# Four table rows, and not two, loaded by SP behind each step of the sums of a graph-attention kernel

## The chip, the core and the metric

The kernel runs on one core of a Trainium2 chip. The core has five engines that work side by side, each through its own queue of instructions in order: TensorE (PE, matrix products; its weight loads are shown apart as PEld), VectorE (DVE), ScalarE (ACT), GpSimd (POOL) and SyncE (SP), which computes nothing and starts transfers. SP, ACT and POOL can all start DMA transfers, which 16 DMA engines carry out. An engine that meets an instruction whose input is not ready stops there, and everything behind it in its queue waits too.

The metric is the time of one execution on the device, in microseconds (us). Three runs of the kernel before took 1981.16, 1981.94 and 1984.87 us; the median is 1981.94 us. One more execution was profiled.

## The reference

The graph has 12,500 nodes with 128 features each and 200,000 edges with 64 features each. The edges come sorted by their target node. The computation is one layer of graph attention with four heads of 32:

```python
h = jnp.maximum(_layernorm(x, axis=-1), 0.0)
h = (node_features @ W_node.T).reshape(num_nodes, H, HD)      # node_features is the h above
e = (edge_features @ W_edge.T).reshape(num_edges, H, HD)
att = jnp.sum(jnp.concatenate([h[src], h[tgt], e], -1) * a, axis=-1)
att = jnp.where(att > 0, att, 0.2 * att)
m = jnp.maximum(segment_max(att, tgt), 0.0)
ex = jnp.exp(att - m[tgt])
denom = segment_sum(ex, tgt) + (num_edges - deg)[:, None] * jnp.exp(-m)
h_prime = segment_sum((ex / denom[tgt])[:, :, None] * h[src], tgt)
out = x + h_prime
```

What matters for this change is `h[src]`: every edge needs the row of its source node, and sources are random. A row holds 137 floats (548 bytes): the four heads' values, four columns of ones, a count and the source's share of the attention logit.

## The kernel before

The edges are cut into groups of 512 places (511 edges and one place for what the group before hands on), four chunks of 128 places to a group (`J`) and four groups to a quad (`QG`). There are 392 groups and 98 quads, numbered 0 to 97. A chunk is 128 rows of the table, one to each partition.

**Stages.** Up to about 100 us the kernel computes the table of node rows in DRAM, while the source inputs of the first four and a half quads are gathered and later converted on the spot. Then it goes over the quads. For each, `all_logits` (L898) makes the attention logits in four steps, one a group; `softmax` (L617) turns the logits of a whole super-quad (two to four quads) into weights; and `sums` (L821) multiplies the gathered rows by the weights and adds them up by target in four steps, with `divide` (L871) for the finished nodes. `together` (L169) interleaves such parts by hand, a step of each in turn: a quad's sums run beside the logits of a quad about five ahead. This order is written out in the code (a manual schedule); no planner moves anything.

**Where the rows come from.** `gather` (L149, its instruction L160) loads one chunk with one indirect DMA, which POOL issues; the rows land in `ga_all`, which has room for eight quads (`QUADS`). So POOL may run ahead of the sums by eight quads and no more.

Some chunks are taken from POOL and loaded row by row, 128 plain DMAs each, by ACT (the last chunk, j = 3, of some groups) and by SP (j = 2). `loaded_by_row` (L714) is a generator: each `next` issues one row's DMA. Which chunks these are is fixed ahead by the rate:

```python
def rows_for(a_quad, j, soonest):                              # L137
    for k in range(nq):
        q = soonest - -(k + 1) * P // a_quad
        if q < nq and quads[q][1] == QG and whole(quads[q][0] + QG - 1):
            by_row[q, QG - 1, j] = k
    return a_quad, j
sync_rows = rows_for((BEHIND_LOGITS + BEHIND_HOT) * QG, J - 2, SYNC_FROM + 6)   # L147
```

With `a_quad` rows a quad, chunk k is that of quad 8 + the rounded-up value of 128 (k + 1) / `a_quad`, as long as this lies below 98. `a_quad` is also the number of addresses that one register load brings to the engine: at every `a_quad`-th row of a chunk `windows` (L507) loads that many byte offsets from `at_row` into SP's registers; a row is then a register move and a DMA (L736). `at_row` is made by one small DVE instruction from `of` (L722, a 512-byte load by SP). The loaded chunk stands in one of three buffers (`ROW_BUFS`), and `take_rows` (L750) lets ACT copy it into `ga` at the head of `all_logits`.

**SP's queue.** SP issues nearly all other transfers, in program order: for each quad the targets `db` (L326, two buffers; each load waits until DVE has read the buffer's last content), the edge features `ea` (L321), and, through `issue` (L519, its DMA L523), four windows of the side table `pw`, four blocks of node inputs `xw` and four blocks of results `out_dram`; for each super-quad the edge order `dr` (L551). A step of the sums issues one `xw`, one `out_dram` and then the rows:

```python
issue("inputs", "results", *(["inputs"] * 3 if q == nq - 3 else []))   # L867, in sums
load_rows(by_sync, q, BEHIND_HOT)                                      # L868
```

A step of the logits issues one `pw` and then `load_rows(by_sync, q, BEHIND_LOGITS)` (L908). In the last step of a quad's logits the `db` of the quad after next comes between. The SP rows begin at quad 2 (`SYNC_FROM`). An `out_dram` waits for DVE's addition of the result (`res`, L892), and that addition waits for the quad's `xw`. The writes of `out_dram` may overlap, so each also waits for the one before to land.

Of the kernel before, what the change touches and what calls it, by code (L numbers as in the profile page):

```python
# [38 lines left out]
QUADS = 8  # L39
ROWS_FROM, ROWS_AHEAD, ROW_BUFS = 6, 7, 3  # L40
BEHIND_COUNT, BEHIND_SUMS, BEHIND_QUAD = 5, 1, 4
SYNC_FROM, BEHIND_LOGITS, BEHIND_HOT = 2, 3, 2
SETS = max(NODE_T, QG * J)
PAD = 1 << 20

# [1172 lines left out]
```

## Time and profile before

| What | Value |
|---|---|
| median of three runs | 1981.94 us |
| the profiled execution's own time | 1978.93 us |
| span in the profile, first to last instruction | 1976.9 us |
| PE, DVE, ACT, POOL busy | 70%, 67%, 22%, 75% of the span |
| chunks gathered by POOL | 1463 from the table, 72 from the inputs |
| rows loaded by ACT, by SP | 2304 (18 chunks), 1664 (13 chunks) |
| granted TensorE clock, mean | 0.539 |

Busy time counts instructions that compute; POOL's indirect DMAs count too, since POOL itself writes their descriptors. Instructions that issue a plain DMA, load a register or wait are not counted, so SP has no busy figure at all: what it does is read from its queue ("SPq" in the rows, "ACTq" for ACT's). In the views of waits a row names the engine and the line that waited, what released it, the sum in us, how often, and the longest. In the timeline a row gives start, duration and what ran; several like instructions in a row are merged, with the small gaps between them, and a time in square brackets is the idle time ahead with its releaser.

### The profile page before, as it was taken

To read this page: it belongs to the slowest core of one execution; us is meant where nothing else is said; L and a number is where in the kernel's file an instruction comes from. 1 tells how busy PE (TensorE), PEld (TensorE's weight loads), DVE (VectorE), ACT (ScalarE), POOL (GpSimd) and SP (SyncE) were. 2 spreads that over 40 slices of the span, in tenths; PEclk is the share of its full clock that TensorE was granted. 3 is DMA by queue.
4 is the path that set the end of the run, shared out by engine and by line. 5 is a ranking of instruction groups with operands and counts; after the bars stand their busy time and mean duration, and the time that the engine had idled before them with its cause. 6 is when DMAs were issued, how large, how long until landed. Compare 5 with 4: busy or idle time off the path is not lost. (4 is left out here: it accounts for less than half of the span.)

```text
span 1976.9 us, 35316 instructions
## 1 busy us (share of the span) xinstructions
PE 1384.9 (70%) x7327; PEld 1247.0 (63%) x7327; DVE 1329.2 (67%) x3297; ACT 426.4 (22%) x1563; POOL 1478.6 (75%) x1578
## 2 busy tenths in 40 slices
PE   6577777777776667667757666667676666777876
PEld 5466777667665656656656565566575655676765
DVE  7676767776775766656747656667576565777876
ACT  6664111211111111111111111111111111111222
POOL 7777777777777777777777777777777777777774
PEclk8877555555555555555555555555555555555557
DMA  7654666566665555565555645555656455565541
GB/s 255 207 146 117 159 153 150 138 151 150 151 156 142 145 138 137 131 144 139 135 138 135 149 123 138 136 143 131 146 129 149 123 149 126 137 153 131 150 103 35
DMA packets 201161, 280.05 MB, mean 142 GB/s; under 512 B 83352, under 2 KB 150839, under 8 KB 193104
## 3 DMA queue, kind: packets, MB, share of 16 engines
q1 hardware_dynamic: 145518, 166.49, 31.6%
q0 software_dynamic: 49120, 107.44, 23.6%
q10 hardware_dynamic: 6306, 3.85, 0.9%
q14 instruction: 156, 1.28, 0.2%
q8 instruction: 61, 1.00, 0.2%
HBM read 254.26 MB, written 23.30 MB: 140 GB/s over the span
## 5 line engine op out<-in xcount | busy, mean ns | idle before, releaser
L160 POOL DMA_INDIRECT ga<-table,srci x1463 | 1391.9, 951 | 448.1 <-issue 389.2
L864 PE MATMUL acc<-ga,hot 128*97 128x137 f32 x2352 | 646.4, 446 | 103.0 <-ACT ga L837 69.9
L864 PEld LDWEIGHTS acc<-ga,hot 128*97 128x97 f32 x2352 | 515.8, 277 | 124.4 <-ACT ga L837 83.6
L575 PEld LDWEIGHTS <-at 80*128 80x128 bf16 x1568 | 213.7, 164 | 384.0 <-DVE at L569 362.2
L578 PE MATMUL lg<-wblk,ea 128*128 128x8 f32 x1568 | 405.9, 356 | 0.0
L575 PE MATMUL lg<-pw,at 80*128 80x12 bf16 x1568 | 169.8, 181 | 314.5 <-DVE at L569 313.3
L578 PEld LDWEIGHTS lg<-wblk,ea 128*128 128x128 f32 x1568 | 378.4, 306 | 0.0
L788 ACT COPY pt<-acc 97x137 f32<-97x137 f32 x392 | 107.4, 274 | 819.2 <-PE acc L787 539.1
L787 PE MATMUL acc<-ga,hot 128*97 128x137 f32 x784 | 261.9, 437 | 27.5 <-ACT ga L785 27.0
L569 DVE TENSOR_TENSOR at<-const_ps,db 80x512 bf16<-80x512 f32 x392 | 267.2, 682 | 8.6 <-DMA db<-in_dst_dram 2.7
L844 DVE TENSOR_TENSOR ga<-ga,ex_ps 128x528 f32<-128x528 f32 x392 | 268.3, 685 | 0.6 <-DVE st L587 0.3
L781 DVE TENSOR_TENSOR ga<-acc,facs 1x132 f32<-1x132 f32 x391 | 115.7, 296 | 207.9 <-ACT pt L788 194.7
L787 PEld LDWEIGHTS acc<-ga,hot 128*97 128x97 f32 x784 | 193.5, 280 | 42.7 <-ACT ga L785 42.1
L599 DVE TENSOR_TENSOR U<-st,ga 128x64 f32<-128x64 f32 x98 | 26.4, 269 | 272.5 <-DMA ga<-table,srci 241.3
L857 DVE TENSOR_TENSOR hot<-const_ps,slot 128x320 f32<-128x320 f32 x384 | 183.1, 477 | 0.0
L785 ACT COPY ga<-acc 1x1 f32<-1x1 f32 x391 | 59.9, 153 | 328.4 <-DVE ga L781 283.0
L892 DVE TENSOR_TENSOR res<-res,xw 80x512 f32<-80x512 f32 (+2 forms) x100 | 67.1, 671 | 44.0 <-DMA xw<-in_x_dram 41.1
L160 POOL DMA_INDIRECT ga<-in_x_dram,srci x72 | 68.8, 956 | 23.1 <-issue 18.3
L888 DVE TENSOR_TENSOR res<-pt,const_ps 80x512 f32<-80x512 f32 (+2 forms) x103 | 67.6, 657 | 4.1 <-DVE const_ps L884 0.3
L691 PE MATMUL ex_ps<-ident,ex 64*128 64x64 f32 (+2 forms) x112 | 18.2, 310 | 53.0 <-ACT ex L678 53.0
L417 PE MATMUL row_ps<-wcat,hT 128*128 128x137 f32 x198 | 38.9, 345 | 21.2 <-DVE tgt L423 9.3
L417 PEld LDWEIGHTS row_ps<-wcat,hT 128*128 128x128 f32 x198 | 33.0, 239 | 26.8 <-ACT hn L248 16.6
(139 smaller groups left out, 1028.4 us busy)
## 6 DMA issues: line engine op xcount, KB each, us to landing
db<-in_dst_dram SPq DMA_DIRECT2D x98, 640.0 KB
ea<-in_edge_t_dram SPq DMA_DIRECT2D x98, 512.0 KB
by_row<-table ACTq DMA_DIRECT2D x2304, 0.5 KB
by_row<-table SPq DMA_DIRECT2D x1664, 0.5 KB
ga<-table,srci POOLq DMA_INDIRECT x1463
xw<-in_x_dram SPq DMA_DIRECT2D x392, 40.0 KB
out_dram<-res SPq DMA_DIRECT2D x392, 40.0 KB
pw<-side SPq DMA_DIRECT2D x392, 1.9 KB
```

What stands on the lines that cost most here:

```text
L160: nc.gpsimd.indirect_dma_start(out=ga[:, i, j, 0:width], out_offset=None, in_=rows, in_offset=bass.IndirectOffsetOnAxis(ap=srci[:, g0 + i, ...
L417: nc.tensor.matmul(row_ps[:, t, :ROW], hT[:, t, :], wcat, start=True, stop=True)
L569: nc.vector.tensor_tensor(at[:, i, :], node_ps[0:SPAN, g0 + i:g0 + i + 1].to_broadcast([SPAN, GE]), db[:, i, :], op=OP.is_equal)
L575: nc.tensor.matmul(lg[:, i, j].rearrange("p k h -> p (k h)"), at[:, i, j * P:(j + 1) * P], sw, start=i + j == 0, stop=False, skip_group_ch ...
L578: nc.tensor.matmul(lg[:, i, 2 * w:2 * w + 2, 0, :], ea[:, i, w, :], wblk, start=False, stop=True, skip_group_check=True)
L781: nc.vector.tensor_tensor(ga[0:1, i, 0, 0:H * HW].rearrange("p (h w) -> p h w", w=HW), before[WIN:WIN + 1, 0:H * HW].rearrange("p (h w) -> ...
L787: nc.tensor.matmul(acc, hot[:, i, 0, :], ga[:, i, 0, :], start=False, stop=True)
L788: nc.scalar.copy(pt[:, i, :], acc)
L844: nc.vector.tensor_tensor(val, val, weight.unsqueeze(3).to_broadcast([P, J, H, HW]), op=OP.mult)
L857: nc.vector.tensor_tensor(hot[:, i, :, 0:SPAN], lane_ps.unsqueeze(1).to_broadcast([P, J, SPAN]), slot[:, g, :].unsqueeze(2).to_broadcast([ ...
L864: nc.tensor.matmul(acc, hot[:, i, j, :], ga[:, i, j, :], start=j == 1, stop=False)
L888: nc.vector.tensor_tensor(res[:, :n, :].rearrange("p g (h d) -> p g h d", d=HD), val[:, :, :, 0:HD], share_ps[0:R, :n, :].unsqueeze(3).to_ ...
```

## The change

A constant is changed: behind each step of the sums SP loads four rows and not two. As a logits step still loads three, `a_quad` for SP becomes (3 + 4) x 4 = 28 and not 20, and by the rule of `rows_for` the chunks that SP loads become nineteen (k = 0 to 18: the last is that of quad 95) and not thirteen. One register load now brings 28 addresses and not 20. The six further chunks, and the places of all nineteen, are left out of what POOL gathers. ACT's chunks stay as they are.

```diff
 BEHIND_COUNT, BEHIND_SUMS, BEHIND_QUAD = 5, 1, 4
-SYNC_FROM, BEHIND_LOGITS, BEHIND_HOT = 2, 3, 2
+SYNC_FROM, BEHIND_LOGITS, BEHIND_HOT = 2, 3, 4
```

## The prediction

> **What bounds the kernel now.** I read the page first. Its chain of work that ended last covers less than 1% of the span and says nothing here, so I went to POOL's timeline, to DVE's waits by stretch, and to SP's queue.
>
> ```profile
> PE 1384.9 (70%) x7327; PEld 1247.0 (63%) x7327; DVE 1329.2 (67%) x3297; ACT 426.4 (22%) x1563; POOL 1478.6 (75%) x1578
> L160 POOL DMA_INDIRECT ga<-table,srci x1463 | 1391.9, 951 | 448.1 <-issue 389.2
> ...
> 1000.96 0.94 POOL L160 DMA_INDIRECT ga<-table,srci  x1 [0.30 <-issue]
> 1002.20 0.94 POOL L160 DMA_INDIRECT ga<-table,srci  x1 [0.30 <-issue]
> 1003.45 0.95 POOL L160 DMA_INDIRECT ga<-table,srci  x1 [0.30 <-issue]
> ...
> 1932.53 0.94 POOL L160 DMA_INDIRECT ga<-table,srci  x1 [0.31 <-issue]
> ```
>
> 75% busy looks like slack, but each chunk has 0.30 us before it that no wait explains: POOL starts a chunk every 1.25 us to its last at 1932.53. POOL is saturated. A quad is 16 chunks less 28/128 for ACT and 20/128 for SP, 15.63 chunks or 19.5 us. Whether the rest keeps up is in DVE's waits, from 257 to 621 us (first two rows) and from 621 to 1720 us (the third):
>
> ```profile
> DVE res L892 <- DMA xw<-in_x_dram: 38.4, 15, 4.8
> DVE U L599 <- DMA ga<-table,srci: 6.0, 2, 5.3
> ...
> DVE U L599 <- DMA ga<-table,srci: 225.4, 37, 10.4
> ```
>
> Two regimes. After 621 us the consumers (PE, DVE, ACT) wait for POOL's rows. Before, they hardly do, and wait for `xw`, which SP loads. POOL began its gathers at the start and is ahead; the consumers catch up. What SP waits for, in the same two stretches:
>
> ```profile
> SPq L523 <- DMA out_dram<-res: 18.9, 25, 2.8
> ...
> SPq L523 <- DVE res L892: 166.2, 49, 6.0
> SPq L523 <- DMA out_dram<-res: 13.8, 23, 1.2
> ```
>
> In the first, SP never waits for DVE, only for its own writes to land; in the second it waits 166 us for DVE. So SP sets the pace of the catch-up. Its pace per quad is the spacing of the `db` loads, one a quad (the number behind x counts them):
>
> ```profile
> L326 SPq DMA_DIRECT2D db<-in_dst_dram x21: 369/416/1210, 257.6 to 604.1; - x21
> 621.18 0.42 SPq L326 DMA_DIRECT2D db<-in_dst_dram  x1
> ...
> 257.57 0.42 SPq L326 DMA_DIRECT2D db<-in_dst_dram  x1
> 273.75 0.41 SPq L326 DMA_DIRECT2D db<-in_dst_dram  x1
> ...
> 281.01 0.56 SPq L736 DMA_DIRECT2D by_row<-table  x2
> 281.67 0.32 SPq L523 DMA_DIRECT2D pw<-side  x1
> 282.08 2.43 SPq L736 DMA_DIRECT2D by_row<-table  x3
> ...
> 286.61 0.87 SPq L736 DMA_DIRECT2D by_row<-table  x3
> 287.57 0.32 SPq L523 DMA_DIRECT2D xw<-in_x_dram  x1
> ...
> 289.53 0.42 SPq L326 DMA_DIRECT2D db<-in_dst_dram  x1
> ```
>
> 21 quads from 257.57 to 621.18 are 17.3 us each. Two clean ones, without `dr` and with hardly a wait, take 16.18 and 15.78 us: SP works all the time. SP therefore needs some 16.3 us of work a quad (17.3 less the 1.0 of waits above, 21 us in 21 quads with the small ones) against POOL's 19.5. That margin of 3.2 us is what the change spends.
>
> **The change, part by part.**
>
> *Off POOL.* Six chunks at 1.25 us: 7.5 us less. If POOL stayed the bound, this would be the whole result; its pace becomes 15.56 chunks, 19.4 us a quad.
>
> *Onto SP's queue, eight rows a quad.* A group of three rows takes 0.87 us and the next entry starts 0.10 later: 0.32 a row. With the stalls that the stretch's rows contain I take 0.34: 8 x 0.34 = 2.7 us.
>
> *The register loads.* They are not counted as busy, and hide in the 2.43 against 0.87 of the groups above.
>
> ```profile
> L509 SPq TENSOR_LOAD <-at_row x91: 526/1448/1632, 128.8 to 1718.9; - x91
> L509 ACTq TENSOR_LOAD <-at_row x90: 1190/1981/2182, 269.3 to 1815.4; - x90
> L729 DVE TENSOR_SCALAR at_row<-of x31: 203/216/460, 128.5 to 1742.1; 1x128 int32<-1x128 int32 x31
> L755 ACT COPY ga<-by_row x31: 287/305/307, 339.4 to 1897.0; 128x137 f32<-128x137 f32 x31
> ```
>
> (minimum, median, maximum in ns). SP's 20 addresses cost 1.45 us, and 8 cost 0.53; ACT already loads 28, for 1.98 (16 for 1.19). A chunk now needs 6 x 1.45 + 0.53 = 9.2 us over 6.4 quads, 1.44 a quad; then 4 x 1.98 + 1.19 = 9.1 over 4.57 quads, 1.99. That is 0.55 more. Fewer loads save nothing, since the price goes by the address.
>
> *Small things.* Six more `of` loads on SP, 0.02 us a quad. Six more `at_row` on DVE (1.3 us) and copies on ACT (1.8 us): beside other work, as DVE idles a third of the span and ACT more; without that cover they would cost those 3.1 us. The bytes moved are the same. A chunk's last row is still issued about three quads before its use, so ACT's wait in `take_rows` stays short.
>
> *SP's pace.* 16.3 + 2.7 + 0.55 + 0.02 = 19.6 us. The waits for landing writes shrink, as two rows (0.65 us) now stand between the writes in addition: the 25 waits average 0.76, and I keep 0.1 to 0.3 a quad. I take **19.7 us**. From below: the mean of the clean quads, 15.98, plus 3.2 (rows at 0.32) gives 19.2; from above: 17.3 with every old wait kept, plus 3.27, gives 20.6. The row nearest is the 21-quad spacing, so I stay near its work, 16.3.
>
> So SP falls behind POOL's 19.4. What is late next is everything that is issued behind the rows: `xw`, on which DVE's addition at L892 waits, then `pw`, `ea` and `db`, for PE and DVE. The consumers never catch up, POOL runs into the eight-quad limit and waits for the sums to free `ga`: its lost 7.5 us buy nothing.
>
> One page weighs the other way. The Trainium skill, DMA: Bandwidth & Descriptors, section "Issuing engines are not separate DMA queues", says that starting DMAs from several engines saves only the sequencer's time, "which is usually small relative to the DMA itself". By that SP's share would not count and the answer would be POOL's saving, the second case below. This trace disagrees about "small": 128 rows and their addresses occupy SP some 53 us, where POOL takes 1.25 us for the chunk.
>
> *The sum.* I date SP's last row, then add the rest.
>
> ```profile
> L736 SPq DMA_DIRECT2D by_row<-table x117: 227/233/287, 130.1 to 256.9; - x117
> L736 SPq DMA_DIRECT2D by_row<-table x420: 227/234/335, 258.1 to 620.5; - x140
> L736 SPq DMA_DIRECT2D by_row<-table x1127: 227/234/922, 621.7 to 1728.7; - x188
> ...
> 239.58 0.37 SPq L523 DMA_DIRECT2D xw<-in_x_dram  x1
> 244.06 0.34 SPq L523 DMA_DIRECT2D out_dram<-res  x1
> ...
> 1804.01 0.27 DVE L599 TENSOR_TENSOR U<-st,ga 128x64 f32<-128x64 f32 x1
> 1829.42 0.27 DVE L599 TENSOR_TENSOR U<-st,ga 128x64 f32<-128x64 f32 x1
> ...
> DVE U L599 <- DMA ga<-table,srci: 5.0, 2, 4.5
> ```
>
> Before 257.57 us SP has issued 117 rows; seven quads of logits made 84 of them and the sums 33, which double: 150. They lengthen the start by 0 to 12 us; waits like the 4.1 us ahead of 244.06 absorb part, so I take 4: SP passes the same place at 262. Of 19 x 128 = 2432 rows 2282 are left, 81.5 quads at 28. At 19.7 us the last row goes out at 262 + 1606 = 1868, not 1728.7. That is in the logits of quad 90.5, which stand between 1804 and 1829 in the trace of before: at 1817, 160 us ahead of the end of the span. In these 160 us the rows are gone, but the consumers have little to gain: the last row above says that from 1800 us on DVE waits only 5 us for POOL. I take 158. Span 1868 + 158 = 2026; with the 2.0 us that the profiled execution has around its span (1978.93 against 1976.9) 2028. The runs' median is 3 us above that execution, within what I can't resolve; I leave 2028.
>
> **The rivals.**
>
> *SP still fits; POOL stays the bound: faster.* It decides at a pace of SP of 19.0, where 262 + 1549 + 158 equals POOL's span of 1969. For it: in the second stretch SP has 3.0 us of waits a quad for DVE (166 us in 56 quads), as much as the change adds. Against it: these waits exist because consumers stand and wait for POOL; that needs the catch-up, which ran on a margin now gone. Time: 1978.93 - 7.5 = 1971.
>
> *SP and POOL tie.* At 19.1 to 19.2 SP loses little more than POOL gains: 1979 to 1986.
>
> *More issue contention.* ACT and SP together issue 56 rows a quad and not 48; single issues of SP's rows already take up to 0.92 us and not 0.23. At 20.5 us a quad: 262 + 1671 + 158 + 2 = 2093.
>
> **How the numbers follow.** Every 0.1 us of pace is 8 us of time. The forecast's case, 19.2 to 20.05, has 0.71 and its own range is 1987 to 2057. POOL-bound has 0.14, the tie 0.05, contention beyond 20.05 has 0.10. The range reaches into the first and the last: 1973 to 2065. Faster by over 0.2% (about what a measurement of this kernel can tell from no change) is 0.13, within it 0.06, slower 0.81.
>
> **What would show it.** Right: `db` loads about 19.7 us apart from 260 us to the end of SP's rows near 1870; hardly a wait of SP for DVE's `res`; DVE waiting for `xw` all along; the 225 us of DVE's wait for gathered rows nearly gone; POOL with idle times over 0.3 us released by PE (acc), where before there is none. Each chunk at 1.25 us still, 1457 of them. Wrong: SP's wait for `res` still there after 700 us, and POOL's last chunk about 7 us earlier. My weakest term is SP's work a quad, whose pieces are tenths of a microsecond, multiplied by 81.5.

## The result, and the profile after

The changed kernel takes 2043.06 us (median of six runs, 2039.74 to 2046.49), the kernel before 1984.28 us beside it (median of six, 1981.16 to 1985.72). The ratio is 1.0305, with a 95% interval of 1.0291 to 1.0319: slower by 3%, where 2028 us was forecast with a range of 1973 to 2065.

From the page of the changed kernel: the span and the engines' busy time, then the groups of POOL's gathers and of DVE's addition of the node inputs, and the rows that SP loads.

```profile
span 2044.7 us, 36881 instructions
PE 1379.1 (67%) x7327; PEld 1246.6 (61%) x7327; DVE 1328.9 (65%) x3303; ACT 427.0 (21%) x1569; POOL 1473.9 (72%) x1572
...
L160 POOL DMA_INDIRECT ga<-table,srci x1457 | 1387.2, 952 | 463.4 <-issue 379.5
...
L892 DVE TENSOR_TENSOR res<-res,xw 80x512 f32<-80x512 f32 (+2 forms) x100 | 67.0, 670 | 345.1 <-DMA xw<-in_x_dram 292.1
...
by_row<-table SPq DMA_DIRECT2D x2432, 0.5 KB
```

All busy sums are as before, within some microseconds, and POOL gathers six chunks less at the same 0.95 us each. Nothing computes longer; the added time is waiting. Where it arises is seen in DVE's waits. The first row is from 257 to 621 us, the other two from 621 to 1880 us:

```profile
DVE res L892 <- DMA xw<-in_x_dram: 70.4, 15, 8.6
...
DVE res L892 <- DMA xw<-in_x_dram: 220.8, 43, 8.5
DVE U L599 <- DMA ga<-table,srci: 0.4, 1, 0.4
```

The first regime of the kernel before, in which DVE waits for `xw`, now lasts to the end of SP's rows. The second, with its 225 us of waits for gathered rows, is gone: the consumers never reach POOL. SP's queue is shown next: a piece of its timeline, its `db` loads, its rows and its address loads, then its waits. The first row of waits is from 257.5 to 1880 us, the second over the whole span, and the last is the same row over the whole span of the kernel before:

```profile
945.61 0.32 SPq L523 DMA_DIRECT2D pw<-side  x1
946.02 2.88 SPq L736 DMA_DIRECT2D by_row<-table  x3
949.00 0.32 SPq L523 DMA_DIRECT2D xw<-in_x_dram  x1
949.41 0.38 SPq L523 DMA_DIRECT2D out_dram<-res  x1
949.88 1.20 SPq L736 DMA_DIRECT2D by_row<-table  x4
951.18 0.32 SPq L523 DMA_DIRECT2D pw<-side  x1
...
L326 SPq DMA_DIRECT2D db<-in_dst_dram x82: 328/416/1051, 265.4 to 1879.0; - x82
...
L736 SPq DMA_DIRECT2D by_row<-table x2432: 225/229/606, 131.3 to 1883.1; - x188
...
L509 SPq TENSOR_LOAD <-at_row x95: 972/1893/2060, 129.5 to 1872.9; - x95
...
SPq L523 <- DMA out_dram<-res: 28.3, 33, 1.9
...
SPq L523 <- DVE res L892: 42.0, 8, 10.4
...
SPq L523 <- DVE res L892: 235.1, 63, 11.1
```

In these lines SP goes from entry to entry with gaps of 0.1 us. 82 `db` loads from 265.4 to 1879.0 are 19.92 us a quad. The wait for `res`, 235 us over the whole span before, is 42 us in 8 places, none of them between 257.5 and 1880 us.

POOL ran into the eight-quad limit, though not often. The stop ahead of the gather at 251.91 us, the first of quad 12, is the first one (`ga` of quad 4 has to be free for it); the last row is POOL's last gather:

```profile
242.91 0.95 POOL L160 DMA_INDIRECT ga<-table,srci  x1 [0.30 <-issue]
251.91 0.94 POOL L160 DMA_INDIRECT ga<-table,srci  x1 [8.06 <-PE acc L787]
...
1942.80 0.94 POOL L160 DMA_INDIRECT ga<-table,srci  x1 [0.31 <-issue]
```

Its last gather is at 1943 us, and the span ends 102 us later; before, 1933 and 44 us. POOL is no longer what the end waits for.

### The profile page after: what moved, and what is told of

The parts are those of the page before. It is cut to its first block, busy times and chain, and to the rows that moved or that the text cites. A ratio compares the mean times of both kernels' runs of the same rounds, so it can differ in the third digit from the quotient of the medians.

```text
span 2044.7 us, 36881 instructions
## 1 busy us (share of the span) xinstructions
PE 1379.1 (67%) x7327; PEld 1246.6 (61%) x7327; DVE 1328.9 (65%) x3303; ACT 427.0 (21%) x1569; POOL 1473.9 (72%) x1572
## 5 line engine op out<-in xcount | busy, mean ns | idle before, releaser
L575 PEld LDWEIGHTS <-at 80*128 80x128 bf16 x1568 | 221.3, 167 | 419.2 <-DVE at L569 395.9
L817 POOL TENSOR_SCALAR hot<-lane,slot 128x80 f32<-128x80 f32 x32 | 15.1, 491 | 46.4 <-issue 28.4
L417 PEld LDWEIGHTS row_ps<-wcat,hT 128*128 128x128 f32 x198 | 30.4, 222 | 28.7 <-ACT hn L248 19.3
```

Of the source, the lines that this page charges most:

```text
L575: nc.tensor.matmul(lg[:, i, j].rearrange("p k h -> p (k h)"), at[:, i, j * P:(j + 1) * P], sw, start=i + j == 0, stop=False, skip_group_ch ...
```

## The experiments

The theory is that SP's time a quad, whatever it is spent on, is the bound. The rivals are the traffic of the added rows on the DMA engines, the longer register load, the place of the rows behind the step of the sums, and the late issue of `xw` alone. In the diffs, three dots stand between pieces of the file that do not follow each other.

**SP's time without any transfer.** The kernel before, its addresses in smaller portions:

```diff
-            at = windows(base_side, 2 * SIDE, g0, m)
+            at = [windows(base_side, 2 * SIDE, g0 + i, 1)[0] for i in range(m)]
...
-            at = ROWS[q] = windows(base_row, 4 * D, g0, m)
+            at = ROWS[q] = [windows(base_row, 4 * D, g0 + i, 1)[0] for i in range(m)]
...
-        by_sync = loaded_by_row(nc.sync, mybir.EngineType.SP, *sync_rows)
+        by_sync = loaded_by_row(nc.sync, mybir.EngineType.SP, 4, sync_rows[1])
```

> The kernel before, with the same transfers and the same 13 chunks, but SP brings its addresses in smaller portions: four rows' addresses to a register load, and one for each block of inputs and of the side table. That adds some 3.2 us of SP's time a quad (about 25 short register loads instead of 5) and no transfer at all. Theory (SP's time is the cause): SP needs 19.5 us and more a quad against POOL's 19.5, the consumers never catch up, 2025 to 2050 us, DVE waits for the node inputs all along. Rival (the added rows' traffic, or contention of the DMA engines, is the cause): nothing changes, 1978 to 1988 us.

Measured: 2032.86 us against 1980.71 us for the kernel before beside it, a ratio of 1.0260 (1.0241 to 1.0280). Its register loads, its `db` loads and DVE's wait:

```profile
L509 SPq TENSOR_LOAD <-at_row x416: 298/552/762, 129.7 to 1789.4; - x139
L509 SPq TENSOR_LOAD <-base_side x392: 260/271/621, 96.5 to 1937.8; - x196
L509 SPq TENSOR_LOAD <-base_row x392: 261/274/743, 137.8 to 1991.3; - x196
...
L326 SPq DMA_DIRECT2D db<-in_dst_dram x77: 327/416/511, 267.5 to 1765.8; - x77
...
DVE res L892 <- DMA xw<-in_x_dram: 302.0, 63, 8.7
```

Not one transfer is added and POOL gathers what it gathered, yet 77 `db` loads stand 19.71 us apart and DVE waits 302 us for `xw`, as in the changed kernel (292). SP's listed waits in this stretch are 0.4 us a quad, so its work is 19.3 us a quad; counted the same way it was 15.8 before. (There are 13 short register loads a quad in place of 3, and not the 25 in place of 5 of the expectation.) This shows that SP's time alone brings a loss of this size; traffic isn't needed for it.

**POOL's half alone.** Six chunks left out of POOL's gathers and loaded by nobody:

```diff
-                if (q, i, j) in by_row:
+                if (q, i, j) in by_row or (i, j) == (QG - 1, 1) and q in (20, 32, 44, 56, 68, 80):
```

> POOL's half alone: the kernel before, SP loading 20 rows a quad, and six chunks (the last group's j = 1 of quads 20, 32, 44, 56, 68 and 80) are not gathered at all, so their edges take stale rows. Theory (POOL is the bound before, at 1.25 us a chunk): 7.5 us less, 0.996 of the time before, 1975 us. If something else than POOL's rate sets the end before, no change.

Measured: 1970.12 us, a ratio of 0.9948 (0.9931 to 0.9964), 10.3 us less with an interval of 7 to 14. The 7.5 us of the prediction lie within it. POOL's last gather, at 1932.53 us before, comes 9.5 us earlier:

```profile
1923.02 0.94 POOL L160 DMA_INDIRECT ga<-table,srci  x1 [0.30 <-issue]
```

POOL's saving was there to be had; SP's share ate it and 59 us more.

**The register load alone.** 20 rows a quad as before, 28 addresses to a load:

```diff
-        by_sync = loaded_by_row(nc.sync, mybir.EngineType.SP, *sync_rows)
+        by_sync = loaded_by_row(nc.sync, mybir.EngineType.SP, 28, sync_rows[1])
```

> The register load alone: 20 rows a quad and 13 chunks as before, but 28 addresses to a register load on SP (five loads a chunk and not seven). Theory (a load costs by the address, 9.1 us a chunk against 9.2): no change, within 0.2% of the time before. Rival (the longer load, 1.9 us in one piece, holds up what stands behind it in SP's queue, or 28 registers cost more): slower by over 0.3%.

Measured: 1.0003 (0.9988 to 1.0018), no change. Its loads and DVE's two waits, over the span:

```profile
L509 SPq TENSOR_LOAD <-at_row x65: 991/1837/1997, 131.0 to 1717.3; - x65
...
DVE U L599 <- DMA ga<-table,srci: 244.4, 43, 11.0
DVE res L892 <- DMA xw<-in_x_dram: 38.2, 13, 5.4
```

There are 65 loads of 1.84 us in place of 91 of 1.45, 111 us in all and not 120: the price goes by the address. DVE's waits are those of the kernel before (241 and 41 us), so the longer piece does no harm. What costs is that the rows, and so the addresses, are more.

**Half the dose.** Three rows behind each step of the sums:

```diff
-SYNC_FROM, BEHIND_LOGITS, BEHIND_HOT = 2, 3, 4
+SYNC_FROM, BEHIND_LOGITS, BEHIND_HOT = 2, 3, 3
```

> Three rows behind each step of the sums: 24 a quad, 16 chunks on SP, POOL 3 chunks fewer than before (3.75 us). Theory (SP's queue is full, the time goes by its work a quad): SP's work is 16.3 + 4 x 0.34 + 0.25 = 17.9 us a quad, with waits some 18.5, under POOL's 19.45. So the consumers still catch up, later than before (near quad 60 to 70 and not 26), and POOL's saving counts: 0.998 of the time before, about 1979 us. Rival (the rows' traffic on the DMA engines, or their place behind the sums, delays the node inputs in proportion to their number): half of what the change lost, about 1.015, 2012 us.

Measured: 1984.37 us, 1.0014 (1.0002 to 1.0026). The rival's 1.015 is out: half the added rows bring a twentieth of the loss, so the loss is not in proportion to the rows. But the gain that was expected did not come either. DVE's waits over the span, `db` loads of the catch-up, POOL at its one long stop, and its gathers:

```profile
DVE U L599 <- DMA ga<-table,srci: 157.1, 31, 8.5
DVE res L892 <- DMA xw<-in_x_dram: 127.2, 34, 7.0
...
L326 SPq DMA_DIRECT2D db<-in_dst_dram x32: 369/416/1510, 414.0 to 996.1; - x32
...
244.39 0.94 POOL L160 DMA_INDIRECT ga<-table,srci  x1 [0.30 <-issue]
253.15 0.94 POOL L160 DMA_INDIRECT ga<-table,srci  x1 [7.81 <-PE acc L787]
...
L160 POOL DMA_INDIRECT ga<-table,srci x1460 | 1396.2, 956 | 455.0 <-issue 380.4 <-PE acc L864 22.9 <-DMA ga<-table,srci 21.4
```

Both regimes are there, the first one longer: SP's pace in it is 18.8 us a quad (31 quads from 414.0 to 996.1 us), under POOL's 19.5, and DVE's waits pass from `xw` to the gathered rows near 1000 us. So the consumers caught up, as expected and somewhat earlier. Why POOL's saving of 3.75 us does not show is open. This profile has a stop of 7.8 us, where POOL reaches the eight-quad limit (the profile of the kernel before has none), and gathers of 956 ns in place of 951, 7 us over 1460. But it is a profile of the slowest of the twelve runs, 1991.58 us, 7 us above their median, and the profile of the register experiment has such a stop too (5.4 us) without a loss in its times.

**Place, order and relief, on slower chips.** The four further kernels ran on other chips (three of them). There the kernel before takes 2692 to 2739 us, so each is set beside the kernel before on its own chip, and the changed kernel itself was run there too. They were not all on one and the same chip, so the ratios are compared across chips. The timeline of SP and two waits of the changed kernel on such a chip:

```profile
1007.22 4.27 SPq L736 DMA_DIRECT2D by_row<-table  x4
1011.52 0.30 SPq L523 DMA_DIRECT2D pw<-side  x1
...
1014.77 3.58 SPq L736 DMA_DIRECT2D by_row<-table  x4
...
1023.58 1.21 SPq L736 DMA_DIRECT2D by_row<-table  x4
...
POOL ga L160 <- PE acc L787: 683.7, 100, 34.4
...
DVE res L892 <- DMA xw<-in_x_dram: 546.0, 60, 15.1
```

Four rows take 1.21 us at one time and 3.58 or 4.27 at another: SP stands still between instructions, by some 0.7 us (346 gaps of 0.6 to 0.8 us from 800 to 1800 us, against 3 on the first chip). POOL waits 684 us for buffers, so POOL is not the bound there. No profile of the kernel before was taken on these chips; that SP was short of time there before the change is likely, not shown. So these chips test whether SP's time counts, but not against POOL's pace. The changed kernel there:

> The changed kernel itself, so that the runs on the slow chips have something to stand beside. On a chip where the kernel before takes some 2700 us: there the kernels with 28 rows a quad took 1.088 (rows behind the logits), 1.072 (inputs a quad earlier) and 1.04 (inputs from ACT's queue). Theory (SP's time is short, there more than elsewhere): the changed kernel between 1.065 and 1.095, so that taking four transfers and a register load a quad off SP wins back about half, and the two others win nothing. Rival (all transfers together count): 1.04, as with the inputs on ACT. On a chip where the kernel before takes 1981 us: 1.03 again.

Measured: 1.0876 (1.0838 to 1.0913), 2927.49 against 2692.09 us.

The place of the rows, five behind the logits' steps and two behind the sums':

```diff
-SYNC_FROM, BEHIND_LOGITS, BEHIND_HOT = 2, 3, 4
+SYNC_FROM, BEHIND_LOGITS, BEHIND_HOT = 2, 5, 2
```

> The same 28 rows a quad, placed otherwise: five behind each step of the logits and two behind each step of the sums. Theory (SP's work a quad counts, not the place): as slow as the changed kernel, 2035 to 2060 us, a little later at the start, since in the quads without sums it loads more rows. Rival (the four rows behind the sums' step come between the node inputs and the results, and that place is the harm): most of the loss gone, under 2000 us.

Measured: 1.0876 (1.0815 to 1.0936), the same as the changed kernel. On these chips the place is not it; on the first one it was not tried.

`xw` a quad earlier (in `sums`; quad 0's are issued at once):

```diff
-            for k in range(nq - 3, nq) if q == nq - 3 else [q] if q < nq - 3 else []:
+            if not q:
+                fetch_inputs(0)
+                issue("inputs", all_of=True)
+            for k in range(nq - 3, nq) if q == nq - 3 else [q + 1] if q + 1 < nq - 3 else []:
```

> The changed kernel with the node inputs loaded one quad earlier, in the same number of transfers. DVE's waits for these inputs (292 us) should go or move elsewhere. Theory (SP is short of time, and the inputs are only where it shows): still 2035 to 2050 us, with the waits moved to other loads or to SP itself. Rival (the inputs are issued too late, and an earlier issue mends it): POOL's bound, about 1975 us.

Measured: 1.0717 (1.0660 to 1.0775). A little is won back, 1.6 of 8.8%, and the waits moved, as this row shows:

```profile
DVE at L569 <- DMA db<-in_dst_dram: 712.0, 70, 21.5
```

Now DVE waits for `db`, 712 us. Putting one load first did not help an engine that is short of time; the next one is late.

SP relieved: `xw` issued from ACT's queue, same transfers, same rows:

```diff
-                    nc.sync.dma_start(*due[kind].pop(0))
+                    (nc.scalar if kind == "inputs" else nc.sync).dma_start(*due[kind].pop(0))
...
+            mine = windows(base_row, 4 * D, g0, m, mybir.EngineType.Activation)
-            due["inputs"] += [(as_bytes(xw[:, i, :]), rows_at(x, at[i], 4 * D)) for i in range(m)]
+            due["inputs"] += [(as_bytes(xw[:, i, :]), rows_at(x, mine[i], 4 * D)) for i in range(m)]
```

> The changed kernel, 28 rows a quad, with the node inputs issued from ACT's queue and not from SP's (four transfers and a register load of four addresses a quad); all transfers are the same. Theory (SP's time is short): SP's work falls from 19.4 by 1.7 to 17.7 us a quad, under POOL's 19.4, the consumers catch up again, and POOL's six chunks count: 1972 to 1982 us. Rival (it is the number of transfers issued by all queues together, or their traffic): as slow as the changed kernel, about 2040 us. ACT has room for 2.3 us a quad; if it has not, its copies of the sums come late and the gain is smaller.

> The changed kernel with the node inputs issued from ACT's queue, once more: the first time it ran on a chip where the kernel before takes 2739 us and all its loads land late, so it could not be set beside the other runs. Theory (SP's time is short): SP's work falls from 19.4 to 17.7 us a quad, under POOL's 19.4, and POOL's six chunks count: 1972 to 1982 us, 0.996 to 1.001 of the time before. Rival (the number or traffic of all transfers): about 1.03.

> The changed kernel with the node inputs issued from ACT's queue, a third time: both times it met a chip where the kernel before takes some 2700 us, because SP's queue stands still for 0.7 us or a multiple of it between many of its instructions. On a chip where the kernel before takes 1981 us the theory (SP's time is short) expects SP's work to fall from 19.4 to 17.7 us a quad, under POOL's 19.4: 1972 to 1982 us, 0.996 to 1.001 of the time before; the rival (number or traffic of all transfers) about 1.03. On a chip of the slow kind I expect 1.04 again, as SP is short of time there even before the change.

Measured: 1.0373, 1.0401 and 1.0395, each within 0.004. Taken alone these lie near the rival's 1.03 (number or traffic of all transfers), and the theory's 0.996 to 1.001, given for a chip of the first kind, was missed. It is the changed kernel's 1.088 on such chips that speaks against the rival: four transfers a quad moved off SP, with their number unchanged, take away more than half of its loss. The register load stays on SP, as the results need its addresses (ACT makes one more), so what SP is relieved of is the four transfers. An earlier issue of `xw` alone won back 1.6%. The kernel still stays behind the one before, and DVE's largest wait is for `db`, as with the earlier `xw` (the row is from the third run):

```profile
DVE at L570 <- DMA db<-in_dst_dram: 572.1, 66, 16.9
```

Whether this version passes the kernel before on a chip of the first kind was asked and not answered: it ran on none.

28 rows only from quad 40 on:

```diff
-SYNC_FROM, BEHIND_LOGITS, BEHIND_HOT = 2, 3, 4
+SYNC_FROM, BEHIND_LOGITS, BEHIND_HOT = 40, 3, 4
```

> No rows on SP before quad 40, then 28 a quad: 10 chunks on SP, 3 more than before on POOL (3.75 us). The consumers have caught up with POOL long before quad 40, so SP's waits of 3 us a quad for DVE stand ready to be used. Theory (19.9 us of SP a quad against POOL's 19.4, wherever they stand): from the sums of quad 40 to about quad 88 SP falls behind by 0.5 us a quad, some 20 us, part of it won back after the last row: 1990 to 2010 us. Rival (SP's excess harms only while the consumers catch up; afterwards the waits cover it): 1984 us, POOL's three chunks alone.

> No rows on SP before quad 40, then 28 a quad, once more for the same reason. Theory (19.9 us of SP a quad against POOL's 19.4, wherever they stand): 1990 to 2010 us, 1.004 to 1.014 of the time before. Rival (SP's excess harms only while the consumers catch up; afterwards its waits cover it): 1984 us, 1.002, for POOL's three chunks alone.

Measured: 1.0228 (1.0185 to 1.0271) and 1.0197 (1.0167 to 1.0227). Both times had been given for a chip on which POOL is the bound once the consumers have caught up. Here it is not: in the second of these runs, before any row on SP, 19 `db` loads from 588.5 to 1026.4 us stand 24.3 us apart, where POOL's 16 chunks take 20 at 1.25 us each.

```profile
L326 SPq DMA_DIRECT2D db<-in_dst_dram x19: 322/323/328, 588.5 to 1026.4; - x19
```

So the runs don't tell the two apart. It stays open whether on the first chip the consumers, once they have caught up, could bear the 28 rows: SP's pace of 19.9 us a quad lies above POOL's 19.4, its work without the waits, 19.0, below. None of the versions that load every row beat the kernel before.

## Why the prediction was right, point by point

- **POOL is the bound before, at 1.25 us a chunk.** Right: six chunks less, with nothing else changed, are 10.3 us (7 to 14) for 7.5 forecast.
- **SP sets the pace of the catch-up and has 3.2 us a quad to spare.** Right that SP sets it and that the room is small: with 3.5 us more of SP's work a quad (15.8 to 19.3) and no transfer, the kernel is 2.6% slower; with 24 rows a quad, 18.8 us of pace, the consumers still catch up. The 3.2 us themselves are not shown, as they set SP's work against POOL's pace and leave out SP's waits.
- **SP's work before, 16.3 us a quad.** This rests on a misreading that did no harm. The prediction took 21 us of waits out of the 21 quads; all waits of SP listed from 257.5 to 621.2 us before add up to 31.5 us, 18.9 for its landing writes and 12.6 for other engines. So the work was 15.8. The same waits for other engines are 46.4 us in the 81.5 quads after: 0.6 a quad both times. Counted as work before, they came along unchanged, and the two errors cancel.
- **The rows' and addresses' cost, 3.27 us a quad.** Right as far as rows can tell. All listed waits after are 74.7 us, 0.9 a quad, so SP's work rose from 15.8 to 19.0, by 3.2. The 28 addresses cost 1.89 us on SP, where ACT's 1.98 had been taken.
- **The waits for landing writes that remain, 0.1 to 0.3 us a quad.** This is the term that was mis-sized. They did shrink, from 0.9 a quad to 0.35 (28.3 us), but 19.7 had little more than 0.1 of them in it. That is the 0.22 us by which the pace of 19.92 misses 19.7.
- **The sum.** SP passes the first mark at 265.4 (262 forecast), issues its last row at 1883.1 (1868), and 161.6 us follow (158). The span is 2044.7 where 2026 was forecast, and the three errors have one sign: 3 at the mark, 12 by the pace, 4 at the end. The 0.22 us would be 18 us over 81.5 quads; but the last row came 81.2 quads of pace after the mark, which takes 6 back. The median, 2043.06, is 3 us below the profiled run, so it misses the forecast by 15.
- **What is late next.** Right: `xw`, 292 us of DVE's waits. That it is only the first in line is shown, on a slower chip, by the run with `xw` earlier, where `db` takes its place.
- **POOL runs into the eight-quad limit.** Right in kind, small in size: nine stops of 19 us in all, 8 of them in the first; POOL's and SP's paces are only half a microsecond apart. The end is set by the consumers 102 us behind it, and not by POOL's stops.
- **The rivals.** That SP still fits needed a pace of 19.0; it is 19.9. That issues contend more is out: a row's median is 229 ns after, 234 before. The Trainium skill's "usually small relative to the DMA itself" (DMA: Bandwidth & Descriptors, section "Issuing engines are not separate DMA queues") does not hold for rows of 548 bytes: in this trace the packet of a row takes its DMA engine 29 ns in the median, and its issue takes SP 229. The run that adds only SP's time gives 2033 us, where by that sentence nothing would have changed.

## What to carry to other kernels

An engine that only issues transfers has no busy figure, and may be nearly full all the same: take a stretch in which it waits for nobody, divide by the loop's count, and compare that, its remaining waits included, with the pace of the bound before giving it more. Its waits for other engines later on are no proof of room, if the others only stand there because it let them catch up. And moving a load off a saturated engine can pay only up to the point where the receiving queue's time for each unit of work reaches the bound's; here half the dose, below that point, neither paid nor cost more than 0.3%, and the whole dose, above it, cost 3%.

## What the runs showed of the hardware that was not expected

On three chips SP paused by some 0.7 us between instructions, 346 times in a millisecond of the changed kernel, and 275 of these times in front of an instruction that waited for nothing the profile shows; in the changed kernel's profile on the first chip no gap of that length stands in front of such an instruction. ACT's queue has such pauses too, 65 in the same millisecond, and none on the first chip. The kernel before took some 2700 us there and not 1981. What makes the pauses is not known from these runs. A register load on SP costs by the address: 0.27 us for one, 0.55 for four, 1.45 for 20, 1.89 for 28.
